# A convolution, FFT-attention and fp8 feed-forward kernel: a new table of issue times, late folding of weights, and smaller clears

## The chip, the cores and the metric

The kernel runs on one core of a Trainium2 chip. A core has four compute engines, each of which works through its own instructions in program order: TensorE (PE, matrix products; its weight loads are shown as PEld), VectorE (DVE), ScalarE (ACT) and GpSimd (POOL). SyncE (SP) issues DMA transfers; ACT can issue some too. Engines wait for each other through semaphores. Matrix products land in PSUM, a small memory that DVE and ACT read; everything else on the chip lies in SBUF. The metric is the device time of one execution in microseconds. The time before is the median of three runs.

## The reference

The input is a batch of 64 images of 96 channels and 56 × 56 pixels. Two layers follow each other.

```python
# layer 0: convolution
out = silu(bn(einsum('bchw,oc->bohw', x, expand_w)))        # 96 -> 192 channels
out = channel_shuffle(shift_groups(out), groups=4)          # quarters shifted by one pixel up/left/down/right
dw  = bn(depthwise_3x3(out)); idb = bn(out * id_w)
out = silu(merge_bn(dw + idb))
se  = relu(grouped_1x1(mean(out)));  se = sigmoid(grouped_1x1(se))
x   = silu(bn(einsum('bchw,oc->bohw', out * se, proj_w)) + x)

# layer 1: on tokens t (3136 x 96 per image)
h = relu(bn(ln(t) @ w1.T))                                  # 192
X = fft(h, axis=tokens)
xr = relu(X.real*rd - X.imag*idg + rb); xi = relu(X.imag*rd + X.real*idg + ib)
t = t + bn(ifft(xr + 1j*xi).real @ w2.T)
h = relu(q_acc(q_acc(q8(ln(t)) @ q8(W1).T) + q8(b1)))       # 384, fp8 e5m2 products, fp16 sums
t = t + q_acc(q_acc(q8(h) @ q8(W2).T) + q8(b2))
```

## The kernel before, in words

The program works image by image and overlaps about four images. The work on an image is cut into 65 kinds of steps, defined as small functions; a kind has from 1 to 21 steps per image. Each step issues a few instructions on one engine. The names below end in `_mm` for PE, `_ev` for an eviction from PSUM by ACT or DVE, `_ld` and `_st` for transfers.

**Order.** The order is written out by hand. A table `PLAN` gives each step of an image a time, and `PERIOD` is added for every next image. Before the kernel is built, all steps of all images are sorted by `b * PERIOD + PLAN[step][i]` and issued in that order (the loop at L990). The times are only keys for the sort: what counts is the order that they give to each engine's queue. Nothing reorders instructions later. An engine stands at the instruction at the head of its queue until that one's operands are there, and everything behind it stands as well. SP's queue, in which nearly all transfers are issued, works in the same way.

**One image, in the order of its data.**

- `x_in` loads the image in seven pieces into the single buffer `xi`. `ea_mm` (L400) expands 128 of the 192 channels in seven row blocks, and ACT's `ea_ev` (L405) evicts them into `e_a`. `eb_mm` (L415) and `eb_ev` (L426) do the other 64 channels into `e_u`, from which four DMAs (`eb_sh`, L438) make the shifted `e_b`.
- The depthwise convolution is shared. `dw_mm` (L468) does most rows of `e_a` on PE: 9 taps × 4 strips × 4 channel blocks = 144 matmuls into four PSUM tiles, read from all of `e_a`, so the first of them waits for the last of the seven `ea_ev`. `gt` (L487, L489) does the remaining rows on DVE and `lt` (L500, L502) the channels of `e_b` on DVE, nine taps each. `dw_ev` (L477), `gs` and `ls` are ACT's evictions; they also sum for the SE gate.
- The gate: `se1_mm` (L512), `se1_ev` (L519), `se2_mm` (L528 and L536), then `se2_ev`, `se2_th`, `se2_pw`, which scale the projection weights. `pj_mm` (L568, L573, L579), `pj_add` (L587, residual, DVE) and `pj_ev` (L593, ACT) write the tokens to `t_buf`, a ring of three images.
- Layer norm: `c_mm` (L623) transposes, `c_st` and `c_v` make the variance, `c_pow` (L650) is a power −1/2 on POOL, `sp_v`, `sp_mm`, `sp_ev`, `sp_st` write it back as one more row of the tokens.
- Attention: `w1_mm` (L681) and `w1_ev` (L686, DVE) multiply with W1. `f1_mm` (L701), `f1_ev` (L713, ACT), `f1_st` (L721) do the first DFT stage in seven parts and store the result to DRAM (`spec`). `f2_ld` (L731, L733) brings it back in another layout into `buf_g`, in four loads. Ahead of the loads 1 to 3 stands a tiny transfer on the same queue, the probe (L731), which reads from what the load before brought: it holds the queue until that load has landed. `f2_mm` (L745, L755) is the second DFT stage in six parts, and `f2_u` (L770, ACT), `f2_s` (L786, L789, DVE), `f2_r` (ACT), `f2_p` (L799, DVE) multiply with the filter and apply the two relus. `w2_mm` (L810, L822) and `w2_ev` (L840) multiply with W2; `i1_mm` (L849), `i1_ev`, `i1_st` do the first inverse stage, through DRAM again (`rows`); `i2_ld` (L873, L874), `i2_mm` (L884), `i2_ev` (L896, DVE) do the second and add to the tokens.
- Feed-forward: `n_mm`, `n_sq`, `n_v`, `n_pow` (L912, POOL) and `n_x` (L919, ACT) normalise seven groups of tokens to fp8; `x_mm` (L926) and `x_ev` (L933) turn them. `h_mm` (L939), `h_ev` (L944), `h_b` (L949, DVE), `h_q` (L955) are the 21 blocks of the hidden layer; `o_mm` (L961), `o_ev` (L966), `o_b` (L971), `o_f` (L977, DVE), `o_st` (L982) are the seven of the output.

**PSUM.** There are two buffers for wide results (`psa`; `w1_mm`, `f1_mm`, `f2_mm`, `w2_mm`, `i1_mm`, `i2_mm` alternate between them) and four for all others (`psb`).

**Setup (L200 to L365).** The weights are loaded, most of them by SP, the rest by ACT. `row_fold` (L213 to L224) loads a batch norm's four rows, takes a square root on ACT and makes scale and shift on DVE; these are folded into the weights: first `ex_w` (L228), later `proj_w` (L304), W1 (L311 to L320, with one matmul of its own at L318), W2 (L323), and the fp8 copies of the feed-forward weights and biases (L328 to L344). POOL clears `e_a`, `e_b`, `e_u`, the three `t_buf` (L351), `buf_h` (L354) and `buf_g` (L360) from end to end. All this is issued ahead of the first image's steps.

Of the kernel before, what the change touches and what calls it, by code (L numbers as in the profile page):

```python
# [7 lines left out]
F32 = mybir.dt.float32  # L8
# [7 lines left out]
C = 96  # L16
# [28 lines left out]
PERIOD = 105.0000000  # L45
PLAN = {
    "x_in": (-5.6038637, -8.8381554, 6.2538794, 1.1812168, 16.3290193, 18.2852724, 6.8664140),
    "ea_mm": (71.3166402, 9.9626057, 70.7451177, 21.6750117, 65.3314579, 73.1081582, 53.0001125),
    "ea_ev": (71.4998900, 11.8833092, 70.9831361, 25.0494290, 65.3324579, 75.4760214, 54.7839542),
    "eb_mm": (20.7568939, 18.2862724, 20.0880579, 17.7349364),  # L50
    "eb_ev": (23.7980033, 19.7804381, 20.6194508, 17.7359364),
    "eb_sh": (30.1373485, 40.4268576, 27.1837130, 37.9131670),
    "eb_z": (47.6742308,),
    "dw_mm": (77.9546249, 77.9556249, 80.7234624),
    "dw_ev": (84.6664508, 84.5735370, 85.4255761, 84.6664508),
    "gt": (
        72.3773055, 76.5125929, 80.2867409, 80.6441083, 81.5978867, 83.3027644, 84.6020247, 85.5619425, 86.6358385,
    ),
    "gs": (87.3111062,),
    "lt": (  # L60
        47.4152368, 51.7884497, 60.4614124, 63.7966655, 70.3566676, 70.7623183, 72.0563386, 78.2533320, 82.6592559,
    ),
    "ls": (84.0968675,),
    "se1_mm": (88.1632442,),
    "se1_ev": (88.3332823,),
    "se2_mm": (89.5466763,),
    "se2_ev": (90.4665288,),
    "se2_th": (90.7934716,),
    "se2_pw": (92.0502895,),
    "pj_mm": (94.5530355, 94.5540355, 102.0867331, 102.0877331),  # L70
    "pj_add": (95.2755331, 97.5636980, 96.0830143, 95.1836140, 106.8994545, 105.9451741, 104.6876054, 105.6968155),
    "pj_ev": (95.9050131, 100.2006242, 96.8964656, 97.4087014, 107.1621768, 108.5177420, 105.3642695, 105.8415338),
    "c_mm": (108.8639612, 112.5088807, 112.0440542, 109.4090967, 116.6350776, 116.2904132, 135.7736125),
    "c_st": (109.9566474, 113.8485179, 113.0437550, 111.6043666, 127.2877074, 117.1026522, 137.4879453),
    "c_v": (113.8495179, 141.3061112),
    "c_pow": (113.8505179, 141.3071112),
    "sp_v": (118.0429167, 144.9541062),
    "sp_mm": (119.0531042, 154.1921897),
    "sp_ev": (120.1871679, 157.1439845),
    "sp_st": (130.9824656, 157.1449845),  # L80
    "w1_mm": (140.5452441, 132.6482511, 135.8336192, 137.4906636, 166.3523765, 171.4972169, 172.4722919),
    "w1_ev": (143.0235958, 134.1359263, 138.9251145, 141.6196817, 167.5676600, 175.3749595, 176.4038215),
    "f1_mm": (145.6274382, 150.9380879, 155.6433445, 167.0161422, 169.8440182, 175.7343775, 181.4398534),
    "f1_ev": (147.8032262, 153.3968496, 159.4311586, 168.6496602, 170.8773139, 175.7353775, 183.1217269),
    "f1_st": (156.9268876, 156.9278876, 159.7610134, 170.1776408, 177.2523722, 181.0963765, 183.4782115),
    "f2_ld": (187.2815556, 187.2825556, 187.2835556, 188.6871659),
    "f2_mm": (191.1567314, 194.9032982, 192.7760178, 198.9093529, 201.4926219, 207.3412304),
    "f2_u": (
        191.1577314, 191.6562889, 197.1245553, 197.1783541, 193.2014504, 193.4636961, 199.3778915, 199.4257855,
        202.6220676, 205.9228992, 210.6728919, 211.5690444,  # L90
    ),
    "f2_s": (
        192.4250284, 193.9349638, 197.4091017, 197.4101017, 194.5789035, 195.6210358, 199.5749065, 199.8323547,
        205.9228992, 207.2409149, 211.9521364, 211.9531364,
    ),
    "f2_r": (193.9359638, 199.3441286, 197.3984294, 206.6372292, 207.5062232, 214.4127396),
    "f2_p": (196.9933570, 199.5074020, 198.4889191, 207.7927174, 209.1210238, 217.7061307),
    "w2_mm": (200.3894916, 200.0698788, 211.3168798, 219.8206887),
    "w2_ev": (201.9237699, 200.2428780, 213.5686424, 221.6127349),
    "i1_mm": (203.1484168, 217.0192486, 223.8701013),  # L100
    "i1_ev": (207.4757051, 209.2393192, 221.2926416, 218.5724351, 226.9503254, 225.7919736),
    "i1_st": (227.4371665, 231.7746699, 237.1127120),
    "i2_ld": (247.3246163, 258.4005613),
    "i2_mm": (247.3256163, 248.9786662, 258.4015613, 258.4015613),
    "i2_ev": (248.8862636, 249.1565727, 251.6982706, 252.2464870, 259.1359643, 258.4025613, 264.6426220, 261.8850697),
    "n_mm": (253.7316943, 255.9231087, 254.3994689, 265.3165318, 262.8490081, 267.4335438, 274.2854929),
    "n_sq": (253.7326943, 256.4684950, 254.9830489, 267.2212265, 263.8196833, 269.2996327, 274.6498815),
    "n_v": (253.7336943, 257.7773358, 255.3268787, 271.2717974, 268.7188670, 272.3139830, 278.4419729),
    "n_pow": (253.7346943, 262.7040095, 256.0602786, 275.1413670, 271.5489182, 273.1976811, 278.5569536),
    "n_x": (259.5582250, 262.7050095, 260.5027085, 276.7536912, 273.5135570, 275.1181728, 279.4588576),  # L110
    "x_mm": (259.5592250, 267.5155107, 260.5037085, 277.7892684, 276.4517499, 277.1023738, 280.0425162),
    "x_ev": (262.4788526, 271.3250083, 262.9497100, 279.9343023, 277.5776996, 279.5752541, 280.9231813),
    "h_mm": (
        282.1072054, 281.8171435, 284.3242143, 283.3068688, 297.0889770, 299.9198326, 301.6559190, 316.8088320,
        330.1509260, 345.7814283, 348.2910018, 350.2353211, 296.8878517, 323.5297033, 341.8803208, 341.1070144,
        349.1164583, 347.9208679, 316.7096209, 337.5767067, 324.7962443,
    ),
    "h_ev": (
        284.9055256, 281.8181435, 286.7711359, 286.2538800, 300.1659528, 301.6061574, 301.6569190, 319.9246149,
        331.0399476, 346.4058862, 354.2442780, 353.1416746, 297.2413855, 326.1086749, 343.4780845, 342.6875640,  # L120
        356.9377387, 352.1488917, 318.6795915, 341.2226048, 328.4873812,
    ),
    "h_b": (
        285.4467375, 285.0084677, 291.2143255, 290.3869640, 307.4021554, 308.1480888, 315.5861436, 337.9149029,
        341.4422638, 351.7638454, 354.2452780, 353.3258891, 302.2808169, 326.8831223, 346.3774903, 342.6885640,
        357.2985996, 352.4379170, 320.6635037, 341.2236048, 337.0905654,
    ),
    "h_q": (
        290.1888952, 290.1898952, 292.3650273, 291.6620769, 314.5146883, 319.2434525, 328.1869035, 340.6025047,
        344.9455204, 354.3021981, 356.7052110, 375.6421815, 326.8831223, 326.8841223, 346.3869475, 346.7213238,  # L130
        374.1067707, 366.6357739, 325.5334877, 345.8789179, 337.3330982,
    ),
    "o_mm": (297.2153719, 323.2068041, 391.0564841, 383.7794044, 346.7502251, 401.7878092, 346.4614096),
    "o_ev": (299.2426704, 325.5592410, 392.9287695, 385.0364968, 346.9425985, 404.8006504, 346.4624096),
    "o_b": (302.4327810, 325.5602410, 395.0955840, 397.1802374, 347.8135349, 407.2015543, 351.0696253),
    "o_f": (325.1830475, 327.1074074, 398.6818786, 400.3662261, 357.3959208, 411.4278754, 351.6615662),
    "o_st": (340.2945764, 339.2746723, 424.0034698, 405.1739043, 379.1046584, 427.6733014, 390.2778445),
# [4 lines left out]
def conv_attn_ffn(  # L142
# [159 lines left out]


    s = row_fold(proj_row, CP, 128, "pj_row")  # L304
    nc.vector.tensor_scalar(s[:, 0], s[:, 0], 0.5, None, ALU.mult)
    for g in range(NG):
        nc.vector.tensor_tensor(pj_w[:, g, :], pj_w[:, g, :], s[:, 0], ALU.mult)


    w1c = const.tile([CP, MID], F32, name="w1c")  # L310
    s1 = row_fold(bn1, MID, C, "s1")  # L311
    w1s = work.tile([C, MID], F32, tag="sq2", name="w1s")
    gcen = work.tile([C, CP], F32, tag="o32", name="gcen")
    nc.scalar.dma_start(out=w1s, in_=w1_t)
    nc.scalar.dma_start(out=gcen, in_=tab_gcenter)
    nc.vector.tensor_tensor(w1s, w1s, s1[:, 0], ALU.mult)
    ps = psb.tile([CP, MID], F32, tag="psb", name="ps_w1c")
    nc.tensor.matmul(ps, lhsT=gcen, rhs=w1s, start=True, stop=True)  # L318
    nc.vector.tensor_copy(w1c, ps)
    nc.sync.dma_start(out=w1c[GAP : GAP + 1, :], in_=s1[0:1, 1, :])  # L320

# [28 lines left out]
    for i in range(NT):  # L350
        nc.gpsimd.memset(t_buf[i], 0.0)  # L351
# [827 lines left out]
```

## Time and profile before

| What | Value |
|---|---|
| time, median of 3 runs (lowest to highest) | 6433.7 us (6433.02 to 6437.04) |
| time of the profiled execution | 6434.72 us |
| span of that execution in the trace | 6432.9 us |
| mean granted PE clock | 0.984 of full speed |
| share of the span in which DVE, ACT, POOL are busy | 85%, 78%, 18% |
| DMA engines' mean busy share, volume | q1: 41.8%; 772.70 MB in all, 120 GB/s |
| first matmul of PE; first `dw_mm`; last `dw_mm` | 34.58; 47.00; 6220.4 us |
| chain that ended last, by engine | DVE 29%, PE 27%, ACT 13%, POOL 12%, DMA 11%, issue 5% |
| its largest lines | L912 8%, L489 7%, the load of `rows` (L874) 6%, L650 4%, L849 4% |

The span runs from the first to the last instruction in the trace; the time of the execution also holds what lies around it. Busy times are of one engine each and overlap. In a group of instructions the page gives the busy time, the mean duration of one in ns, then the idle time of the engine just ahead of them, and what ended most of it. In a timeline each line is a run of like instructions: its start, how long they last, engine, line, operation and, in brackets, the idle time before it with what ended it. The chain by engine is spread over all of them: in this kernel work of four images interleaves, and each engine hands over to the next many times in an image.

### The profile page before, as it was taken

Reading aid. Unit: us, or ns where it says so; the run is one execution under the profiler, and the core shown is the slowest. Engines: PE = TensorE matmul, PEld = TensorE weight load, DVE = VectorE, ACT = ScalarE, POOL = GpSimd, SP = SyncE. Lnnn points to the kernel's source line nnn. Section 1 sums busy time; section 2 is a strip of 40 time slices with the busy share of each in tenths; the row PEclk is TensorE's granted clock in tenths of the full one; section 3 lists DMA queues with packets and bytes.
Section 4 is the critical chain, followed back from the end, with each engine's and each line's share of the span. In section 5 each row is a group of like instructions: output and inputs, shape, how many; then the busy total and the mean of one; then the engine's idle time right before and its main releaser. Section 6 shows DMA issues by size and latency. Waiting matters only on the chain.

```text
span 6432.9 us, 215622 instructions
## 1 busy us (share of the span) xinstructions
PE 5903.3 (92%) x92162; PEld 3939.1 (61%) x92162; DVE 5452.4 (85%) x10386; ACT 5003.9 (78%) x10830; POOL 1159.1 (18%) x652
## 2 busy tenths in 40 slices
PE   5999999999999999999999999999999999999996
PEld 3666666666666666666666666666666666666664
DVE  6788888888888888888988888888888888888885
ACT  2677778778777787777787787878877877878777
POOL 1112112112112111121121121211211211211211
PEclk8999999999999999999999999999999999999997
DMA  3344434444444444344444443443443444444433
GB/s 93 109 117 127 125 110 133 122 118 127 121 122 127 115 127 125 110 131 119 117 129 123 121 126 113 130 121 113 132 125 112 130 124 117 127 117 129 121 108 92
DMA packets 665511, 772.70 MB, mean 120 GB/s; under 512 B 273104, under 2 KB 591256, under 8 KB 664424
## 3 DMA queue, kind: packets, MB, share of 16 engines
q1 hardware_dynamic: 661832, 757.14, 41.8%
q8 instruction: 724, 11.86, 0.8%
q10 hardware_dynamic: 2720, 1.77, 0.1%
q14 instruction: 235, 1.93, 0.1%
HBM read 349.05 MB, written 354.16 MB: 109 GB/s over the span
## 4 chain that ended last, share of the span: by engine, by line
DVE 29%; PE 27%; ACT 13%; POOL 12%; DMA 11%; issue 5%; SPq 2%; POOLq 0%; DVEq 0%; ACTq 0%
POOL rs L912 8%; DVE d_vec L489 7%; DMA buf_g<-rows 6%; POOL rs L650 4%; PE psa L849 4%; DMA buf_g<-spec 4%; DVE t L896 3%; DVE d_last L502 3%; DVE ue L789 3%; DVE s L786 3%; ACT ue L770 3%; PE ps_pj L568 3%; PE psa L810 2%; PE ps_pj L579 2%; PE ps_eb L415 2%
## 5 line engine op out<-in xcount | busy, mean ns | idle before, releaser
L650 POOL TENSOR_TENSOR rs<-v,mhalf 128x16 f32<-128x16 f32 (+1 forms) x128 | 384.7, 3006 | 4385.6 <-DVE v L645 4385.6
L955 ACT CAST h<-y 128x448 fp8e5<-128x448 f16 x1344 | 749.0, 575 | 286.8 <-DVE y L949 286.8
L502 DVE SCALAR_TENSOR_TENSOR d_last<-e_b,taps,d_last 128x1568 f32<-128x1568 f32 x512 | 944.0, 1844 | 0.5
L912 POOL TENSOR_TENSOR rs<-v,mhalf 128x4 f32<-128x4 f32 x448 | 741.7, 1760 | 818.9 <-DVE v L617 784.0
L489 DVE SCALAR_TENSOR_TENSOR d_vec<-e_a,taps,d_vec 128x1120 f32<-128x1120 f32 x512 | 707.1, 1381 | 2.7
L949 DVE TENSOR_SCALAR y<-y,qb 128x448 f16<-128x448 f16 x1344 | 424.9, 329 | 324.8 <-ACT y L944 318.0
L944 ACT CAST y<-ps_h 128x448 f16<-128x448 f32 x1344 | 674.6, 539 | 26.9 <-PE ps_h L939 26.9
L681 PE MATMUL psa<-w1c,t 112*128 112x192 f32 x3584 | 669.0, 330 | 2.8 <-DMA t<-dev_t 2.8
L468 PE MATMUL ps_d<-e_a,diag 32*32 32x504 f32 x18432 | 628.6, 590 | 1.5 <-issue 1.4
L681 PEld LDWEIGHTS psa<-w1c,t 112*128 112x128 f32 x3584 | 592.5, 190 | 22.4 <-ACT fs L713 3.0
L468 PEld LDWEIGHTS ps_d<-e_a,diag 32*32 32x32 f32 x18432 | 410.5, 103 | 200.7 <-ACT y L944 37.3
L745 PE MATMUL psa<-l_tab,buf_g 128*64 128x112 f32 x7424 | 425.3, 267 | 113.9 <-DMA buf_g<-spec 87.9
L745 PEld LDWEIGHTS psa<-l_tab,buf_g 128*64 128x64 f32 x7424 | 369.5, 140 | 250.4 <-DMA buf_g<-spec 131.5
L919 ACT ACTIVATE xt<-ps_n,rs 128x96 fp8e5<-128x96 f32 x1792 | 454.4, 346 | 72.5 <-POOL rs L912 65.9
L686 DVE SCALAR_TENSOR_TENSOR buf_h<-psa,rs 128x768 f32<-128x768 f32 x448 | 425.5, 950 | 55.0 <-PE psa L681 54.6
L977 DVE TENSOR_TENSOR o<-t,o 112x448 f32<-112x448 f32 x448 | 418.8, 935 | 21.8 <-ACT o L971 19.5
L786 DVE SCALAR_TENSOR_TENSOR s<-psa,fa,ue 128x448 f32<-128x448 f32 (+1 forms) x512 | 325.2, 635 | 117.3 <-ACT ue L770 112.8
L593 ACT ACTIVATE t<-ps_pj,pjbn_b 112x504 f32<-112x504 f32 (+1 forms) x512 | 300.5, 619 | 150.2 <-DVE ps_pj L587 150.2
L400 PE MATMUL ps_ea<-x,ex_w 112*32 112x448 f32 x3584 | 416.1, 550 | 0.0
L770 ACT ACTIVATE ue<-psa,fa 128x448 f32<-128x448 f32 (+1 forms) x512 | 336.5, 686 | 100.0 <-DVE buf_h L799 57.7
L701 PE MATMUL psa<-buf_h,f_tab 56*64 56x384 f32 x3584 | 395.2, 509 | 17.6 <-DVE t L896 9.3
L810 PE MATMUL psa<-w2a,buf_h 128*64 128x96 f32 (+1 forms) x7424 | 358.9, 248 | 50.2 <-ACT buf_g L840 34.0
(171 smaller groups left out, 11865.9 us busy)
## 6 DMA issues: line engine op xcount, KB each, us to landing
spec<-fs SPq DMA_DIRECT2D x448, 384.0 KB
buf_g<-spec SPq DMA_DIRECT2D x192, 672.0 KB
out_dram<-o SPq DMA_DIRECT2D x448, 196.0 KB
buf_g<-rows SPq DMA_DIRECT2D x128, 672.0 KB
x<-in_x SPq DMA_DIRECT2D x320, 203.0 KB
rows<-buf_g SPq DMA_DIRECT2D x128, 420.0 KB
rows<-buf_g SPq DMA_DIRECT2D x64, 504.0 KB
x<-in_x SPq DMA_DIRECT2D x128, 228.4 KB
```

The lines of the kernel that those rows point to most:

```text
L468: nc.tensor.matmul(pss[r][j * 32 : j * 32 + 32], lhsT=diag[pr, tap, :], rhs=e_a[pr, r0 : r0 + SR, dx : dx + HW], start=tap == 0, stop=tap ...
L489: nc.vector.scalar_tensor_tensor(d_vec, win, w, d_vec, ALU.mult, ALU.add)
L502: nc.vector.scalar_tensor_tensor(d_last, win, w, d_last, ALU.mult, ALU.add)
L650: nc.gpsimd.tensor_tensor(rs[:, js], v[:, js], mhalf[:, js], ALU.pow)
L681: nc.tensor.matmul(ps[:, k, 0:MID], lhsT=t[:, n0 : n0 + 2 * TP], rhs=w1c, start=True, stop=True)
L745: nc.tensor.matmul(ps[c0 : c0 + 64, k, 0:CP], lhsT=g_v[:, k1, c0 : c0 + 64], rhs=l_tab[:, k1, :], start=True, stop=True,)
L770: nc.scalar.activation(held["ue", b, i][:, q, 0:n, :], held["f2", b, i][:, 0:n, 0:HW], AF.Identity, bias=par[:, 2 + q : 3 + q], scale=par[ ...
L786: nc.vector.scalar_tensor_tensor(held["s", b, i][:, q, 0:n, :], im, par[:, m : m + 1], a, ALU.mult, ALU.add)
L810: nc.tensor.matmul(ps[c0:c1, u, k, 0:C], lhsT=pq_a[:, AT[k1], c0:c1], rhs=w2a, start=k == 0, stop=False, skip_group_check=True,)
L912: nc.gpsimd.tensor_tensor(rs, held.pop(("nv", b, g)), mhalf[:, 0:4], ALU.pow)
L944: nc.scalar.copy(y16, held.pop(("h", b, i)))
L955: nc.scalar.copy(held["h8", b, j][:, m, :], held.pop(("y", b, i)), saturate=False)
```

## The change

It has four parts.

1. `PERIOD` and all times of `PLAN` are new. The same steps with the same instructions are issued, in another order.
2. The folds of `proj_w`, W1, W2 and the fp8 copies, with their loads, one matmul and one SP transfer, become a function `late()`. It is called once inside the loop, ahead of the first step that is a `dw_mm`, `gt` or `lt`. In the new table the first image's four `eb_mm`, `eb_ev` and `eb_sh` and its `ea_mm` and `ea_ev` 6 stand ahead of that step (`x_in` issues nothing for the first image, whose loads are in the setup).
3. `t_buf` and `buf_g` are cleared only where nothing writes later (pad columns, and the end), `buf_h` not at all.
4. `f2_mm` contracts over the 112 partitions that the loads fill, in place of all 128.

```diff
-PERIOD = 105.0000000
+PERIOD = 109.6727979
 PLAN = {
...
-    "ea_mm": (71.3166402, 9.9626057, 70.7451177, 21.6750117, 65.3314579, 73.1081582, 53.0001125),
-    "ea_ev": (71.4998900, 11.8833092, 70.9831361, 25.0494290, 65.3324579, 75.4760214, 54.7839542),
+    "ea_mm": (29.8923641, -0.8291959, 15.0300743, 18.1271558, 16.1520669, 22.7063896, -38.1683085),
+    "ea_ev": (29.9777652, 2.2743661, 15.5665715, 18.8637647, 18.1436194, 22.7073896, -37.4821034),
...
-    "dw_mm": (77.9546249, 77.9556249, 80.7234624),
+    "dw_mm": (30.3928279, 30.3938279, 34.0920719),
...
-    "f1_mm": (145.6274382, 150.9380879, 155.6433445, 167.0161422, 169.8440182, 175.7343775, 181.4398534),
+    "f1_mm": (92.2829535, 99.4674191, 103.0707832, 117.9381640, 122.0957825, 128.8107291, 132.7282313),
...
-    "f2_ld": (187.2815556, 187.2825556, 187.2835556, 188.6871659),
-    "f2_mm": (191.1567314, 194.9032982, 192.7760178, 198.9093529, 201.4926219, 207.3412304),
+    "f2_ld": (144.7372912, 146.8339830, 148.8356832, 150.0693909),
+    "f2_mm": (145.3563533, 147.8344004, 147.3263213, 150.4141302, 155.3866585, 164.7888946),
...
-    "i2_ld": (247.3246163, 258.4005613),
-    "i2_mm": (247.3256163, 248.9786662, 258.4015613, 258.4015613),
+    "i2_ld": (187.2178098, 203.6176020),
+    "i2_mm": (194.5481398, 194.8859899, 205.0557761, 210.4045313),
...
-    "n_pow": (253.7346943, 262.7040095, 256.0602786, 275.1413670, 271.5489182, 273.1976811, 278.5569536),
-    "n_x": (259.5582250, 262.7050095, 260.5027085, 276.7536912, 273.5135570, 275.1181728, 279.4588576),
+    "n_pow": (200.5048950, 207.2348271, 216.3540908, 218.6861280, 231.7969976, 227.8823828, 235.5603406),
+    "n_x": (212.1782382, 214.0214340, 217.7449647, 225.8208361, 234.0563002, 231.4551848, 238.0110459),
...
-    s = row_fold(proj_row, CP, 128, "pj_row")
-    nc.vector.tensor_scalar(s[:, 0], s[:, 0], 0.5, None, ALU.mult)
...
     w1c = const.tile([CP, MID], F32, name="w1c")
...
+    def late():
+        s = row_fold(proj_row, CP, 128, "pj_row")
+        nc.vector.tensor_scalar(s[:, 0], s[:, 0], 0.5, None, ALU.mult)
+        for g in range(NG):
+            nc.vector.tensor_tensor(pj_w[:, g, :], pj_w[:, g, :], s[:, 0], ALU.mult)
+
+        s1 = row_fold(bn1, MID, C, "s1")
+        w1s = work.tile([C, MID], F32, tag="sq2", name="w1s")
+        gcen = work.tile([C, CP], F32, tag="o32", name="gcen")
+        nc.scalar.dma_start(out=w1s, in_=w1_t)
+        nc.scalar.dma_start(out=gcen, in_=tab_gcenter)
+        nc.vector.tensor_tensor(w1s, w1s, s1[:, 0], ALU.mult)
+        ps = psb.tile([CP, MID], F32, tag="psb", name="ps_w1c")
+        nc.tensor.matmul(ps, lhsT=gcen, rhs=w1s, start=True, stop=True)
+        nc.vector.tensor_copy(w1c, ps)
+        nc.sync.dma_start(out=w1c[GAP : GAP + 1, :], in_=s1[0:1, 1, :])
+
+        s = row_fold(bn2, C, 128, "s2")
...
+        nc.vector.tensor_copy(eye8, eye.rearrange("p (d a) -> p d a", a=TP)[:, :, 0:HW], saturate=False)
+        fw1 = work.tile([C, HID], F32, tag="sq2", name="fw1")
+        nc.scalar.dma_start(out=fw1, in_=ffn_w1)
+        nc.vector.tensor_copy(q1, fw1, saturate=False)
...
-        nc.gpsimd.memset(t_buf[i], 0.0)
+        nc.gpsimd.memset(t_buf[i].rearrange("p (b a) -> p b a", a=TP)[:, :, HW:TP], 0.0)
...
-    nc.gpsimd.memset(buf_h, 0.0)
...
-    nc.gpsimd.memset(buf_g, 0.0)
+    nc.gpsimd.memset(buf_g[:, 2 * NK * C :], 0.0)
...
-                        lhsT=g_v[:, k1, c0 : c0 + 64],
-                        rhs=l_tab[:, k1, :],
+                        lhsT=g_v[0:CP, k1, c0 : c0 + 64],
+                        rhs=l_tab[0:CP, k1, :],
...
     with tc.manual_schedule():
+        first = True
         for _, b, k, i in sorted(
...
         ):
+            if first and STEPS[k] in (dw_mm, gt, lt):
+                late()
+                first = False
             STEPS[k](b, i)
```

## The prediction

> **What bounds it now.** First the page's busy row: TensorE is busy 92% of the span.
>
> ```profile
> PE 5903.3 (92%) x92162; PEld 3939.1 (61%) x92162; DVE 5452.4 (85%) x10386; ACT 5003.9 (78%) x10830; POOL 1159.1 (18%) x652
> ```
>
> So 6432.9 − 5903.3 = 529.6 us of PE idleness, 8.2 us for each of 64 images, is all that a new order can win. Next the L468 groups by image: the first depthwise starts at 47.0 us, the last at 6220.4, so an image takes (6220.4 − 47.0) / 63 = 98.0 us on average; a tail of 212.5 follows. I take an undisturbed image, 31 (L468 at 3085.5 to 3182.0, 96.5 us), and time everything from its L468. Third, PE's timeline, for where it stands still:
>
> ```profile
> 3098.11 0.73 PE L961 MATMUL ps_o<-h,q 128*112 128x448 fp8e5 x3
> 3099.80 1.75 PE L745 MATMUL psa<-l_tab,buf_g 128*64 128x112 f32 x32 [0.97 <-DMA buf_g<-spec]
> ...
> 3102.58 0.50 PE L528 MATMUL ps_se<-red,ep_w 24*32 24x1 f32 x40 [0.54 <-ACT red L519]
> ...
> 3107.85 3.65 PE L568 MATMUL ps_pj<-d,pw 32*112 32x504 f32 x32
> ...
> 3116.54 1.53 PE L810 MATMUL psa<-w2a,buf_h 128*64 128x96 f32 x32 [0.89 <-ACT buf_g L840]
> ...
> 3129.91 0.98 PE L623 MATMUL ps_c<-eye,t 112*128 112x112 f32 x8 [0.93 <-ACT t L593]
> ```
>
> No wait rules; half a dozen of 0.3 to 1 us do. The largest single one is for the spectrum's second load; over the run the page's groups put 87.9 + 131.5 = 219 us to it, weight loads included, which partly overlap:
>
> ```profile
> L745 PE MATMUL psa<-l_tab,buf_g 128*64 128x112 f32 x7424 | 425.3, 267 | 113.9 <-DMA buf_g<-spec 87.9
> L745 PEld LDWEIGHTS psa<-l_tab,buf_g 128*64 128x64 f32 x7424 | 369.5, 140 | 250.4 <-DMA buf_g<-spec 131.5
> L468 PE MATMUL ps_d<-e_a,diag 32*32 32x504 f32 x18432 | 628.6, 590 | 1.5 <-issue 1.4
> ```
>
> The third row counts as much: today the depthwise never waits at its start. Fourth, the DMA queue's timeline of that load chain:
>
> ```profile
> 3086.49 0.36 SPq L721 DMA_DIRECT2D spec<-fs  x1
> 3089.16 0.32 SPq L733 DMA_DIRECT2D buf_g<-spec  x1
> 3094.34 0.60 SPq L731 DMA_DIRECT2D probe<-buf_g  x1
> 3095.03 0.33 SPq L733 DMA_DIRECT2D buf_g<-spec  x1
> 3099.78 0.58 SPq L731 DMA_DIRECT2D probe<-buf_g  x1
> ```
>
> The last store goes 1.0 after L468, and the second load is seen landed (the second probe) at 14.25. The chain hangs on f1_mm 6 (L701), which in this image starts at 3181.22 before L468 at 3182.02, 0.8 earlier. So: 14.25 + 0.8 = 15.06 us from f1_mm 6 to the second load.
>
> **The new table, per image.** Instruction counts do not change, so only waits do. I walked the built order by hand with the start-to-start times of the trace (ACT: f1_ev 0.69, o_ev 0.42, h_ev 0.45, ea_ev 0.55; DVE: f2_s pair 1.2, f2_p pair 1.07, gt 1.30; PE steps as in the timeline).
>
> *Depthwise entry, a new wait.* PE now runs f1_mm 6, o_mm 5, four h_mm, ea_mm 0, L468. That is 0.81 + 0.60 + 0.78 + 0.87 = 3.06 us of work. L468 needs ea_ev 0, which stands on ACT behind f1_ev 6, o_ev 5 and four h_ev. f1_ev 6 can start 0.95 after f1_mm 6, and ACT arrives some 0.45 late: 1.40 + 0.69 + 0.42 + 4 × 0.45 + 0.55 = 4.9. **PE stands 1.8 us** (1.35 if ACT is on time). Behind L468 on PE is the whole filter phase, and dw_ev, the gate and the projection wait for it, so nothing hides this.
>
> *Load chain, a wait removed.* f1_mm 6 now leads L468 by 4.9 instead of 0.8. The second load lands at 15.06 − 4.9 + 0.85 (o_st 4, now ahead of the first load on the SP queue: issue 0.4, and f1_ev 6 0.45 late) = 11.0, or 12.5 if o_st 4 must wait for its data. f2_mm 2 comes at 13.5, so the 0.97 goes. Next late is ACT: o_mm 0 just ahead needs h_ev 12, which ends at 12.9. The SP queue then has o_st 2 before the third probe; it waits for o_f 2 at about 12.1 and more, so load 2 is issued near 13.4 and lands at 18.4 to 19.4 (5.0 to 6.0 as above); f2_mm 3 wants it at 19.25. Level; priced 0.
>
> *L468 to projection (L568).* Before 3107.85 − 3085.5 = 22.3. After: f2_mm 2 to 15.2, the SE sums ready at 15.4, f2_mm 1 to 17.85, f2_mm 3 to 20.95 (0.4 waiting), **21.2**: −1.1.
>
> *L568 to LN transposes (L623).* Before 3129.91 − 3107.85 = 22.1. After, the filter's ACT/DVE pairs interleave (f2_u 3 behind f2_s 2, f2_u 7 behind f2_s 6), the second w2_mm waits 1.0 for f2_s 7 in place of the 0.89 in the view, f2_mm 5 waits for f2_s 9, and L623 follows the last pj_ev more closely: 43.55 − 21.2 = **22.35**: +0.3.
>
> *L623 to the next L468.* Before 52.1, in which I count 2.4 of waits (rows 0.9, x_mm's normalised tokens 0.5, powers behind o_mm 3 0.45, L849 0.25, sp_mm 0.3), so 49.7 of work. The powers:
>
> ```profile
> L919 ACT ACTIVATE xt<-ps_n,rs 128x96 fp8e5<-128x96 f32 x1792 | 454.4, 346 | 72.5 <-POOL rs L912 65.9
> ```
>
> ACT waits 65.9 us for them. The new table puts 7 to 12 us of other work between n_pow (1.76 on average) and its n_x, so these go, and DVE's idleness before sp_v hides behind PE's expansion. The rows stay: PE reaches the third i2_mm at 69.05, and the second load of rows, whose issue now stands behind o_st 0, lands at about 70: 1.0. With the 1.8 at the entry: 49.7 + 1.0 + 1.8 = **52.5**: +0.4.
>
> Sum 21.2 + 22.35 + 52.5 = 96.1 against 96.5: −0.4. The walk alone gives 94.6; 0.5 of hand-offs that the same walk misses before, and the rows' 1.0, are in the 96.1.
>
> *Disturbed images.* The mean is 98.0 − 96.5 = 1.5 above image 31, from late loads and from the clock. The windows of an image with a slow clock and of 31, in the same phase:
>
> ```profile
> 2013.70:2023.70 10.00, 8.85 (x160) 6.95 (x158) 8.88 (x15) 7.95 (x17) 0.00 (x0) 0.83 0.50 134
> 3099.50:3109.50 10.00, 8.52 (x170) 6.65 (x174) 9.31 (x16) 8.47 (x17) 0.00 (x0) 1.00 0.50 135
> ```
>
> 0.83 (the third column from the end) over 10 us is 0.17 × 10 / 0.5 = 3.4 us at half clock. I found such a stretch in about 19 of 58 images, each after gaps of at most 1.3 us, at about 0.8 us each. The Trainium skill ("TensorE: Matmul & The Clock Gate", section "🎯 Why this matters for your kernels") tells to avoid idle gaps over some 3 us, one idle window bringing half clock. By that rule the 1.8 at the entry is safe and costs its wait alone. By the row, shorter pauses do it, and here full-rate depthwise work stands behind: up to 1.7 us in every image, 107 us in all. The trace decides: I take 0.4 per image (a quarter of 1.7), 0.5 for loads still late: 0.9 instead of 1.5, −0.6 (bounds 0 and −1.5).
>
> Per image −0.4 − 0.6 = −1.0; 63 intervals: **−63 us**.
>
> **Start.** Before, PE's first matmul comes at 34.6, behind the fold of W1. Afterwards the expansion matmuls (L415, one L400) can start near 23.8, when the folded weights' row has landed (issued at 21.6). But the folds come behind these evictions on ACT, with nine DMAs issued by ACT and two more activation-table loads (1.28 each). The W1 product follows at about 41, and L468 at 47.5: no gain there. The first large-channel tap (L500), today at 50.7 behind the e_b transfers, can go at 45.3, and the first projection follows that much earlier: **−6** (bounds 0 and −12). If the folds' loads lag, w1c is still not needed for tens of us.
>
> **Memsets, 112 rows.** POOL's clears end at 25.1, before anything reads those buffers; shorter ones give 0, and nothing else was hidden under them. Contracting over 112 instead of 128 partitions streams the same 112 columns: L745's 267 ns stays, 0. Tail: same steps, 0 ± 5.
>
> Sum: profiled execution 6434.7 (span 6432.9 + 1.8 around it) − 63 − 6 = **6366**. It lies 1.0 above the median 6433.7.
>
> **Rivals.** (1) The walk without its additions: rows in time, clock full, hand-offs hidden: 94.6 + 1.2 of disturbance = 95.8, −2.2 per image, 6434.7 − 6 − 139 = **6290**. For it: the loads gain 4 us. Against: before, the bare walk fell short by 0.5. (2) Mere exchange: the entry wait returns what the load wait gave, or the plan's reordering is hidden under PE anyway: only the start is gained, **6428**. For it: PE is 92% busy; against: several waits shrink, not one. (3) **Slower: the depthwise entry decides.** If ACT reaches f1_ev 6 another 0.9 late (two h_ev more) and every pause halves the clock (1.7 instead of 0.4), the entry costs 2.2 more: +1.2 per image, 6434.7 − 6 + 76 = **6505**. It decides once entry and clock together cost over 3.2 us per image (1.8 + 0.4 counted, 1.0 won). For it: 3.4 us at half clock would lie on the depthwise's 9.7, and nowhere else do seven ACT instructions stand in front of a PE start. Against: dense PE work around it.
>
> **Chances.** Forecast 0.40 (own range 6320 to 6415), walk bare 0.16, exchange 0.10, slower 0.34. 0.2% (13 us) is about what this measurement tells from no change. Forecast and bare walk are faster: 0.56; exchange same: 0.10; slower 0.34. The range goes from 6280, just below the bare walk, to 6520, just above the slow case.
>
> **What would show it.** Right: L745's waits for the spectrum near 0; a new idle of about 1.8 × 63 = 115 us before L468, released by ACT's e_a (L405); L919's wait for POOL near 0; L884's for rows at 60 us or so; L468 to L468 at 97.0; first L500 near 45. Wrong if the entry idles over 3 us, if half-clock stretches appear in most images, if the load wait stays, or if DVE's filter chain leaves w2_mm waiting far over 1 us.

## The result and the profile after

The changed kernel takes 6476.9 us (median of four runs, 6469.39 to 6501.28), against 6433.6 before (four runs): 1.0073 times, 95% interval 1.0044 to 1.0101. It is slower, where 1% less was forecast; it lies inside the range. The profiled execution, 6469.39 us with a span of 6467.4, is the fastest of the four. The rows below are of it, where nothing else is said. Its line numbers are two lower than before from the steps on (L743 for L745).

The page's busy row and the groups that answer to those of before:

```profile
PE 5899.3 (91%) x92162; PEld 3883.6 (60%) x92162; DVE 5482.9 (85%) x10386; ACT 5003.4 (77%) x10832; POOL 1095.6 (17%) x651
...
L466 PE MATMUL ps_d<-e_a,diag 32*32 32x504 f32 x18432 | 631.2, 590 | 55.4 <-ACT e_a L403 50.3
...
L917 ACT ACTIVATE xt<-ps_n,rs 128x96 fp8e5<-128x96 f32 x1792 | 469.2, 362 | 62.1 <-POOL rs L910 62.1
L743 PE MATMUL psa<-l_tab,buf_g 112*64 112x112 f32 x7424 | 418.4, 264 | 88.5 <-DVE ue L787 74.3
...
L882 PE MATMUL psa<-r_tab,buf_g 64*48 64x56 f32 x14336 | 353.9, 214 | 85.3 <-DMA buf_g<-rows 80.4
```

PE's work is the same; the idleness around it is 568 us instead of 530. L743 no longer names the spectrum, L466 has a wait that it didn't have, and L917 still waits 62.1 us for powers, where the forecast had none. PE's waits summed (line, releaser, us in total, times, longest):

```profile
PE psa L808 <- DVE ue L787: 102.5, 64, 3.8
PE psa L882 <- DMA buf_g<-rows: 80.4, 62, 3.1
PE psa L743 <- DVE ue L787: 74.3, 124, 2.2
PE ps_d L466 <- ACT e_a L403: 50.3, 64, 0.8
...
PE ps_n L599 <- ACT xt L917: 39.6, 57, 0.7
...
PE psa L743 <- DMA buf_g<-spec: 9.7, 4, 7.2
```

The same list of before, cut to the spectrum's and the rows' matmuls:

```profile
PE psa L745 <- DMA buf_g<-spec: 87.9, 76, 8.4
...
PE psa L884 <- DMA buf_g<-rows: 43.7, 51, 2.8
...
PE psa L745 <- DVE ue L789: 25.4, 42, 2.2
```

The spectrum's wait has gone, but at the same matmul the wait for VectorE's filter chain (`ue`) has grown from 25.4 to 74.3 us, and the rows' wait has nearly doubled.

By depthwise starts, the first stands at 43.5 us (47.0 before), the first image takes 84.6 (88.9), each later one 98.74 on average (98.14), and the tail is 217.2 (212.5): −3.5 − 4.3 + 62 × 0.61 + 4.6 = +34.6, which is the difference of the spans (34.5) but for rounding. Cut at the same three places as the forecast, means over 59 images from the fifth on (the forecast's column is for an undisturbed image; its 0.9 us for disturbed ones is not in it):

| stretch | before | forecast | after |
|---|---|---|---|
| L468 to projection | 23.2 | 21.2 | 21.8 |
| projection to LN transposes | 21.9 | 22.35 | 22.5 |
| transposes to next L468 | 53.0 | 52.5 | 54.6 |

The first two came within 0.6 us of the forecast. The third took 2 us more. The fastest tenth of the images takes up to 96.9 us in both kernels: an undisturbed image gained nothing, where 0.4 was forecast, and the mean lies 1.9 us above that, where it lay 1.2 above before. The chain of waits shows its course in one image (start, us, what):

```profile
3052.47 6.19 DMA buf_g<-rows
3058.66 0.04 issue
3058.71 1.43 PE psa L882 x54
...
3062.62 0.94 ACT xt L917 x4
3063.57 0.03 POOLq L910
3063.60 0.10 issue
3063.69 3.14 POOL rs L910
3066.83 0.02 issue
3066.85 0.04 ACT xt L917
...
3067.94 1.54 PE ps_n L599 x32
```

Second load of rows; i2_mm 2; the first n_x; then a power of 3.14 us on POOL; n_x 2, which frees the PSUM buffer for which n_mm 5 waits. POOL's and VectorE's timelines of that moment, in two fences:

```profile
3063.69 5.54 POOL L910 TENSOR_TENSOR rs<-v,mhalf 128x4 f32<-128x4 f32 x2 [3.07 <-ACT xt L917]
```

```profile
3062.78 0.17 DVE L615 TENSOR_SCALAR v<-v 128x4 f32<-128x4 f32 x1
3063.04 1.16 DVE L894 SCALAR_TENSOR_TENSOR t<-psa,bn2c_b,t 112x392 f32<-112x392 f32 x2
3064.11 1.84 DVE L500 SCALAR_TENSOR_TENSOR d_last<-e_b,taps,d_last 128x1568 f32<-128x1568 f32 x1
```

The variance (L615) is there at 3062.95. The power starts only at 3063.69, released by ACT's xt: its result has two buffers, and the first is held until n_x 0 has read it. By then one of the depthwise's nine passes on VectorE, a tap (L500), is due, and the power ends 0.88 after the tap.

### The profile page after: what moved, and what is told of

It is laid out like the page before. It is cut to its first block, busy times and chain, and to the rows that moved or that the text cites. A ratio compares the mean times of both kernels' runs of the same rounds, so it can differ in the third digit from the quotient of the medians.

```text
span 6467.4 us, 214988 instructions
## 1 busy us (share of the span) xinstructions
PE 5899.3 (91%) x92162; PEld 3883.6 (60%) x92162; DVE 5482.9 (85%) x10386; ACT 5003.4 (77%) x10832; POOL 1095.6 (17%) x651
## 4 chain that ended last, share of the span: by engine, by line
PE 53%; ACT 16%; DVE 15%; DMA 10%; POOL 3%; issue 2%; SPq 0%; ACTq 0%; POOLq 0%; DVEq 0%
PE ps_d L466 9%; DMA buf_g<-rows 8%; PE psa L679 6%; DVE ue L787 5%; DVE s L784 5%; ACT ue L768 5%; PE psa L699 4%; PE psa L808 4%; PE ps_ea L398 4%; PE ps_n L599 4%; DVE buf_h L797 3%; PE psa L847 3%; POOL rs L910 3%; PE ps_eb L413 2%; ACT d L475 2%; PE ps_c L621 2%
## 5 line engine op out<-in xcount | busy, mean ns | idle before, releaser
L648 POOL TENSOR_TENSOR rs<-v,mhalf 128x16 f32<-128x16 f32 (+1 forms) x128 | 331.8, 2592 | 3941.9 <-DVE v L643 3941.9
L500 DVE SCALAR_TENSOR_TENSOR d_last<-e_b,taps,d_last 128x1568 f32<-128x1568 f32 x512 | 944.2, 1844 | 0.4
L942 ACT CAST y<-ps_h 128x448 f16<-128x448 f32 x1344 | 690.9, 546 | 90.9 <-PE ps_h L937 83.3
L466 PE MATMUL ps_d<-e_a,diag 32*32 32x504 f32 x18432 | 631.2, 590 | 55.4 <-ACT e_a L403 50.3
L466 PEld LDWEIGHTS ps_d<-e_a,diag 32*32 32x32 f32 x18432 | 361.6, 103 | 319.0 <-ACT e_a L403 100.0
L917 ACT ACTIVATE xt<-ps_n,rs 128x96 fp8e5<-128x96 f32 x1792 | 469.2, 362 | 62.1 <-POOL rs L910 62.1
L743 PE MATMUL psa<-l_tab,buf_g 112*64 112x112 f32 x7424 | 418.4, 264 | 88.5 <-DVE ue L787 74.3
L743 PEld LDWEIGHTS psa<-l_tab,buf_g 112*64 112x64 f32 x7424 | 363.2, 137 | 219.5 <-issue 163.1
L808 PE MATMUL psa<-w2a,buf_h 128*64 128x96 f32 (+1 forms) x7424 | 363.6, 250 | 103.0 <-DVE ue L787 102.5
L882 PEld LDWEIGHTS psa<-r_tab,buf_g 64*48 64x48 f32 x14336 | 336.6, 122 | 175.7 <-DMA buf_g<-rows 107.1
L937 PE MATMUL ps_h<-xq,q 96*128 96x448 fp8e5 x1344 | 417.8, 358 | 24.6 <-ACT o L964 18.8
L808 PEld LDWEIGHTS psa<-w2a,buf_h 128*64 128x64 f32 (+1 forms) x7424 | 316.1, 131 | 203.4 <-issue 134.5
L882 PE MATMUL psa<-r_tab,buf_g 64*48 64x56 f32 x14336 | 353.9, 214 | 85.3 <-DMA buf_g<-rows 80.4
```

The source lines that it names most:

```text
L466: nc.tensor.matmul(pss[r][j * 32 : j * 32 + 32], lhsT=diag[pr, tap, :], rhs=e_a[pr, r0 : r0 + SR, dx : dx + HW], start=tap == 0, stop=tap ...
L500: nc.vector.scalar_tensor_tensor(d_last, win, w, d_last, ALU.mult, ALU.add)
L743: nc.tensor.matmul(ps[c0 : c0 + 64, k, 0:CP], lhsT=g_v[0:CP, k1, c0 : c0 + 64], rhs=l_tab[0:CP, k1, :], start=True, stop=True,)
L808: nc.tensor.matmul(ps[c0:c1, u, k, 0:C], lhsT=pq_a[:, AT[k1], c0:c1], rhs=w2a, start=k == 0, stop=False, skip_group_check=True,)
L882: nc.tensor.matmul(ps[oh * 64 : oh * 64 + 48, d, k, 0:HW], lhsT=p_v[pr, g * 7 + k, oh * 48 : oh * 48 + 48], rhs=r_tab[pr, g * 7 + k, :], s ...
L917: nc.scalar.activation(xt[:, k, :], cen[:, k, 0:C], AF.Copy, scale=rs[:, k : k + 1], saturate=False)
```

## The experiments

Each ratio is to the kernel before, run on the same chip. Where a run is set against the changed kernel, the two ratios are subtracted, and the difference carries the changed kernel's interval, ±0.3%, too.

**Which part.** The kernel before with the new `PERIOD` and `PLAN` (e1), and the changed kernel with the old ones (e2, the same lines the other way round):

```diff
-PERIOD = 105.0000000
+PERIOD = 109.6727979
...
```

> The kernel before with the new table alone (folds ahead of the loop, full clears, 128 rows as before). Theory A, the table costs all of it: the span without the start's gain, so 6477 + 8 = about 6485 (first depthwise 3.5 us later and first image 4.3 us longer than in the changed kernel). Theory B, the late folds or the smaller clears cost something in every image: about 6430, as the kernel before.

> The old table with everything else of the change. Theory A, the table costs all of it: the old time, less at most some 4 us of the start, 6430. Theory B, the folds or the clears cost: about 6475.

Measured: the table alone 1.0052 (1.0037 to 1.0068), the rest alone 0.9992 (0.9985 to 0.9999), some 5 us gained. The loss is the table's. Theory A's extra 8 us of the start can't be seen in e1, which lies 0.2% below the changed kernel instead of 0.1% above; the two intervals overlap.

**The power's buffers.**

```diff
-        v = small.tile([128, 4], F32, tag="v2", name="v2")
+        v = small.tile([128, 4], F32, tag="v2", name="v2", bufs=4)
...
-        rs = small.tile([128, 4], F32, tag="rs2", name="rs2")
+        rs = small.tile([128, 4], F32, tag="rs2", name="rs2", bufs=4)
```

> The changed kernel with four instead of two buffers for n_pow's result and its input, so that the third power needn't wait for the first n_x and can run before the tap of the depthwise starts on VectorE. Theory A, the chain from the second load of rows over that power sets the period: the power falls from 3.1 to about 1 us, the 1.0 us wait of n_x 2 and the 0.7 us wait of n_mm 5 go, 0.7 to 1.0 us per image, 6415 to 6435. Theory B, ScalarE's gapless queue up to ea_ev 0 sets it whatever comes in time: within 15 us of 6477.

Measured: 0.9978 (0.9967 to 0.9988), that is 0.95% or 61 us less than the changed kernel. This version is faster than before. POOL's timeline of the same power, and the group of n_x on the page:

```profile
3047.80 1.01 POOL L910 TENSOR_TENSOR rs<-v,mhalf 128x4 f32<-128x4 f32 x1 [3.03 <-DVE v L615]
```

```profile
L917 ACT ACTIVATE xt<-ps_n,rs 128x96 fp8e5<-128x96 f32 x1792 | 468.6, 363 | 0.1
```

The power is released by its input now, takes 1.01 us, n_x waits 0.1 us instead of 62.1, and the wait of L599 is gone from PE's list. Theory A holds. The same edit on the kernel before:

> The kernel before with four buffers for n_pow. Theory A, the shortage of buffers bites only in the new table's order, in which the third power falls beside a tap: 0.998 to 1.000. Theory B, it bites in both orders, and the old table would gain as much by them: about 0.990.

Measured: 0.9978 (0.9967 to 0.9989), just outside A's span and far from B's. The old order loses 0.2% by two buffers, the new one 0.95%. **With four, both tables take the same time**, within the intervals: the new one's loss against the old goes with this wait. The forecast's gain doesn't come with it: 0.9895 times the kernel before was forecast, so some 50 us remain for other terms. (By PE's lists of the two runs the rows cost the new table 41 us more and the filter chain at L743 41 more, and it gains 91 at the spectrum's loads.)

**The rows.** The second load brings one row of fourteen, the rest of what i2_mm reads there is left over, and `buf_g` is cleared in full:

```diff
     def i2_ld(b, h):
         ns = slice(h * 14, h * 14 + 14)
...
+        if h:
+            ns = slice(14, 15)
         nc.sync.dma_start(out=p_v[:, ns, :], in_=held["rows", b][ns].rearrange("n p o -> p n o"))
```

> The changed kernel with one of fourteen rows in the second load of the inverse's rows (13 of 14 stay what the first stage left in the buffer; buf_g cleared in full), so that it lands some 3 us earlier. Theory A, the late rows set the end of the period: the 1.3 to 1.6 us of waiting for them go, 1.2 to 1.6 us per image, 6375 to 6400. Theory B, ScalarE's queue sets it: less than 30 us gained.

Measured: 0.9908 (0.9888 to 0.9927), 1.65% or 106 us less than the changed kernel, a little more than A's best. PE's waits (the edit puts two lines more ahead of these, L884 for L882):

```profile
PE ps_d L466 <- ACT e_a L403: 50.3, 64, 0.8
PE ps_n L599 <- ACT xt L919: 43.7, 62, 0.7
...
PE psa L884 <- DMA buf_g<-rows: 9.7, 12, 1.7
```

The rows' 80.4 fell to 9.7; the entry's 50.3 stands as it was and the power's wait (39.6) is no smaller. So ACT's full queue does not set the period by itself: what comes earlier is passed on. The 106 us are more than the 71 us of PE's wait that went, and the run also moves 41 MB less, 5% of all; how much of the gain is owed to that is not shown.

**Entry against loads.** f1_mm 6 and f1_ev 6 go behind ea_mm 0 and ea_ev 0:

```diff
-    "f1_mm": (92.2829535, 99.4674191, 103.0707832, 117.9381640, 122.0957825, 128.8107291, 132.7282313),
-    "f1_ev": (95.9417072, 101.8812031, 110.6728132, 118.8299838, 124.3453549, 129.3140504, 133.9449543),
+    "f1_mm": (92.2829535, 99.4674191, 103.0707832, 117.9381640, 122.0957825, 128.8107291, 139.9),
+    "f1_ev": (95.9417072, 101.8812031, 110.6728132, 118.8299838, 124.3453549, 129.3140504, 139.95),
```

> The changed kernel with f1_mm 6 and its eviction moved behind ea_mm 0 and ea_ev 0, as the last PE work ahead of the depthwise, as in the kernel before. Theory A, the new table exchanges a wait at the depthwise's entry for one at the spectrum's loads, at par: the entry's 1.55 us falls to about 0.8, and the wait of f2_mm 2 for the second load comes back with 0.7 to 1.0 us: within 20 us of the changed kernel, 0.9967 to 1.003 times its time. Theory B, the entry wait is a plain loss: 40 to 50 us faster than the changed kernel. Theory C, the lead of the loads is worth more than the entry: 30 us or more slower.

Measured: 1.0115 (1.0098 to 1.0131), 0.42% or some 27 us slower than the changed kernel, between A and C. PE's waits:

```profile
PE psa L743 <- DMA buf_g<-spec: 86.7, 77, 8.7
...
PE ps_d L466 <- ACT e_a L403: 0.8, 1, 0.8
```

Both sides moved: the entry's wait on ea_ev 0 goes, the spectrum's comes back at its size of before (87.9). The early f1_mm 6 pays for its entry wait, and for some 27 us more. With the spectrum's waits the clock falls too: the mean granted clock of the profiled execution is 0.979, that of the changed kernel 0.988.

**The filter's pairs.** f2_u 3 ahead of f2_s 2, f2_u 7 ahead of f2_s 6:

```diff
     "f2_u": (
-        145.9574170, 146.0784519, 151.3369770, 151.5443434, 147.5670473, 147.6492190, 152.3936269, 152.7665860,
+        145.9574170, 146.0784519, 151.3369770, 151.3370, 147.5670473, 147.6492190, 152.3936269, 152.3937,
```

> The changed kernel with f2_u 3 issued right behind f2_u 2 and f2_u 7 right behind f2_u 6, ahead of f2_s 2 and f2_s 6, so that ScalarE needn't wait for VectorE within a pair. Theory A, the interleaving delays VectorE's chain by 0.8 us for each pair and the second w2_mm by their sum: its wait of 1.7 us goes, 1.0 to 1.6 us less per image, 60 to 100 us faster than the changed kernel. Theory B, the projection's additions and the rows' transfers catch up behind it: less than 20 us.

Measured: 1.0010 (1.0000 to 1.0020), 0.63% or 40 us less than the changed kernel: two thirds of the least that A gave. PE's waits:

```profile
PE psa L808 <- DVE ue L787: 59.4, 63, 3.5
```

Of 102.5 us 59.4 are left. A pair cost 0.33 us of PE, not 0.8: the two w2_mm take 5.52 us instead of 6.18 and the whole 0.66 reaches the period.

**PE work into the rows' wait.** w1_mm 6 and w1_ev 6 move ahead of i2_mm 2. In e6 and e8 that puts them ahead of sp_st 1 too, which writes one row of what w1_mm 6 reads: the last group is computed with that row's old contents. e9 and e11 put it behind the store:

```diff
-    "w1_mm": (75.0447409, 77.0123629, 83.4039362, 81.8880042, 112.8805086, 123.7822720, 106.4625024),
-    "w1_ev": (76.3003028, 81.6278978, 84.6401265, 84.4029004, 121.6081060, 127.8733347, 117.8451368),
-    "i2_mm": (194.5481398, 194.8859899, 205.0557761, 210.4045313),
+    "w1_mm": (75.0447409, 77.0123629, 83.4039362, 81.8880042, 112.8805086, 123.7822720, 95.9),
+    "w1_ev": (76.3003028, 81.6278978, 84.6401265, 84.4029004, 121.6081060, 127.8733347, 95.92),
+    "i2_mm": (194.5481398, 194.8859899, 205.7, 210.4045313),
```

> The changed kernel with w1_mm 6 and its eviction moved from behind x_mm 0 to ahead of i2_mm 2, into the time in which PE waits for the second load of rows. Theory A, from these rows to the next depthwise PE's own work and the power bound the time: 0.5 to 1.3 us less per image, 30 to 80 us faster than the changed kernel. Theory B, ScalarE's queue behind n_sq 2, which still waits for the rows, bounds it: within 15 us.

> The changed kernel with w1_mm 6 and its eviction moved into the wait for the second rows, this time behind the store of the row that it reads, and i2_mm 2 right behind it. Theory A, the chain from the rows over n_x and the third power sets the period of the changed kernel, not PE's own work: no more than 20 us either way, 1.004 to 1.010 times the kernel before. Theory B, PE's work behind the rows sets it: 1.3 us less per image, about 0.995.

Measured: 1.0378 and 1.0277 (1.0256 to 1.0298). Neither theory had that. PE's waits of e9:

```profile
PE ps_n L599 <- ACT xt L917: 98.0, 64, 1.6
...
PE psa L679 <- DMA t<-dev_t: 63.2, 50, 2.9
```

w1_mm 6 itself was not ready: the row's store, late in SP's queue, lands when PE already waits for it (63.2 us in all). i2_mm 2 behind it starts at 73.3 instead of 71.7 us after L466, w1_ev 6 holds up h_b 9 on VectorE and with it h_q 9, o_b 4 and n_sq 2 on ACT by 1.5 to 2.8 us, and the image takes 101.2 instead of 98.8. So a delay of 1.6 us at i2_mm 2 became 2.4, with a longer wait for n_x's buffer (98.0 us for 39.6) and a granted clock of 0.979 for 0.988. These runs don't tell whether PE's own work bounds the end of the image; that stays open.

**Together.** Buffers and pairs; all three, with w1_mm 6 as in e9; and all three as in e6:

> The changed kernel with four buffers for n_pow and the filter's pairs. Theory A, both are separate waits, and each shortens every image on its own: their gains of 0.95% and 0.63% add, 1.0073 - 0.0158 = 0.9915 times the kernel before. Theory B, what the pairs gain is lost again where the rows are waited for: 0.996 to 0.998, as with the buffers alone.

> Both of these and w1_mm 6 in the wait for the rows, behind the store of its row. Theory A, with the power out of the way PE's own work bounds the end of the image, and work moved into a wait is won: 0.5 to 1.3 us per image below the run with both, 0.978 to 0.987 times the kernel before. Theory B, ScalarE's queue behind the rows now bounds it: within 0.3% of the run with both.

> The changed kernel with four buffers for n_pow, w1_mm 6 ahead of i2_mm 2, and the filter's pairs as in the run before this. Theory A, these are separate waits in three places, whose prices add: 58 (four buffers, measured) + 50 + 80 = some 190 us less than the changed kernel, 6260 to 6310. Theory B, each uncovers the same next limit (ScalarE's queue): 6370 to 6410.

Measured: buffers and pairs 0.9935 (0.9922 to 0.9948), 1.38% less than the changed kernel, where the two alone sum to 1.58. Nearly A: the waits are for the most part separate. This is the best version that computes everything, 6395.5 us, 0.65% faster than before. With w1_mm 6 moved, 1.0007 (e11) and 1.0308 (e8): it costs 0.7% behind the store and far more ahead of it. So with four buffers and the pairs it costs a third of the 2.0% of e9: i2_mm 2 is again 1.6 us later, but only 1.0 of it reaches the period, and the wait of L599 is 22.2 us where e9 has 98.0. Both theories of e11 missed.

## Why the prediction was wrong

The time lies inside the stated range by luck: the range reached so far up for the sake of the slower rival, whose cause did not come.

**Depthwise entry: right, a little less.** PE's timeline ahead of L466:

```profile
3080.99 0.88 PE L699 MATMUL psa<-buf_h,f_tab 56*64 56x384 f32 x8
3081.80 0.78 PE L959 MATMUL ps_o<-h,q 128*112 128x448 fp8e5 x3
3082.41 0.73 PE L937 MATMUL ps_h<-xq,q 96*128 96x448 fp8e5 x3
3083.43 0.35 PE L937 MATMUL ps_h<-xq,q 96*128 96x448 fp8e5 x1 [0.28 <-ACT o L964]
3083.86 0.96 PE L398 MATMUL ps_ea<-x,ex_w 112*32 112x448 f32 x8
3085.61 1.90 PE L466 MATMUL ps_d<-e_a,diag 32*32 32x504 f32 x49 [0.79 <-ACT e_a L403]
```

From L699 to L466 4.62 us (4.9 forecast) with 3.06 of work: 1.55 us of standing, in two places, since the last h_mm waits for a PSUM buffer as well. 1.8 was counted. In PE's list the two waits sum to 50.3 + 18.8 = 69 us, where 115 were to show.

**Loads of the spectrum: right.** 87.9 us of PE became 9.7. (The 219 of the prediction counts weight loads and matmuls for the same waits.) In the same place the wait for the filter chain grew by 49 us.

**Filter chain: right in sum, partly by luck.** The second w2_mm waits 1.6 us (102.5 in 64 images) and not 1.0; other waits of that stretch came out smaller, so the sum fits.

**The powers: the step that failed.** "The new table puts 7 to 12 us of other work between n_pow (1.76 on average) and its n_x, so these go." That compared the places of the two steps in the table, and took the power's average. Even by the table it is not so for the third: n_pow 2 stands at 216.35 and n_x 2 at 217.74, 1.4 apart. In the trace the seven powers start 3.0 to 5.1 us ahead of their n_x on average, which is enough for all but the third. It didn't ask when the third power may start: with two buffers, after n_x 0. Nor what runs on VectorE then: of the 448 powers of the changed kernel 200 have no tap beside them, and 197 of these take 1.01 us; the 125 that start within a tap take about 2.4 and end 0.86 after it; 56, the third of nearly every image, take 3.1. The wait cost ACT 1.0 and PE 0.6 us per image, where nothing was counted; without it the kernel is 0.95% faster. That accounts for the sign. Of the forecast gain that is still missing, about 0.8 us per image, the next terms explain a part.

**The rows: mis-sized.** 1.0 us per image was counted. The two waits of i2_mm take 1.5 on average; that of i2_mm 2 lies between 0 and 3.3, and behind long ones the clock falls. The windows at the same phase of an image with such a pause, and of one without (the third column from the end is the granted clock):

```profile
1970.60:1980.60 10.00, 7.65 (x159) 5.91 (x159) 6.43 (x15) 4.55 (x10) 2.16 (x3) 0.83 0.55 132
2071.90:2081.90 10.00, 10.00 (x218) 7.60 (x216) 9.34 (x19) 8.90 (x25) 3.17 (x4) 1.00 0.58 149
```

10 of 58 images have this, most of them behind waits of 2.1 us and more: 0.34 us per image over all. The mean image lies 1.9 us above the fastest tenth, where the forecast allowed 0.9 above an undisturbed image. The four runs reach from 6469 to 6501 us while their mean granted clock falls from 0.988 to 0.984; why it falls is open. With its 0.9 the forecast gives an image 97.0 us; 98.8 are measured. The powers (0.7: the image of e3's profiled execution takes 98.1), the rows (0.5) and their slow clock (0.3), less the entry's 0.25, make some 1.3 of these 1.8; the rest was not attributed: the 49.7 us of work in the third stretch were an estimate.

**The clock at the entry: forecast too high.** 0.4 us was added for half clock behind the pause, and up to 1.7 in the slower rival. In 58 images no window of the first 10 us behind L466 is below full clock. In the filter phase 18 of 58 were so before and none is now. Here the rule of the Trainium skill weighed above (gaps of some 3 us) was the better guide, though less can do it: the rows' pauses of 2.1 us show it, and the filter phase before, where 14 of the 18 stretches follow pauses of at most 0.83 us. (The other four follow 2.0 to 2.6 us, so the prediction's "at most 1.3" did not hold for all.) The slower rival named the sign, but not the place: its entry costs less than counted.

**Start and end.** First depthwise and first image together gained 7.8 us (6 forecast), 3.5 of them at the first depthwise, where none was forecast. The first tap of `lt` starts at 41.0, not 45.3. The tail lost 4.6, within the 5 allowed.

## What to carry to other kernels

When an order is changed, ask of each short step on the path not only how far its reader stands behind it, but from when it may start: the buffer of its result is a wait too. Price it by the duration that it has beside its new neighbours, not by its average. A wait in a stretch where every queue is full is not filled by moving work ahead unless that work's own operands are there.

## What the runs showed of the hardware

A power on POOL of 128 × 4 numbers takes 1.01 us with no tap beside it; one that starts within a tap on VectorE ends 0.86 us after that tap (125 of 125). The Trainium skill ("SBUF — State Buffer", section "🔬 SBUF: two separate sides") says that a VectorE instruction with two SBUF inputs, as a tap is, and a GpSimd one that reads SBUF lock each other out for the whole instruction, whichever starts first keeping the port. The blocking agrees. The order doesn't quite: the third power starts 0.42 us ahead of its tap and is still held up, 56 times, while 67 others that start 0.12 to 0.82 ahead of a tap take 1.01, and the taps keep their 1.84. The lead alone does not decide it: in e11 61 powers that start 0.43 to 0.47 us ahead of a tap take 1.01. Why is open; moving a tap alone was not tried.
